# Who copies the table while the nodes are ranked: the first stage of a graph transformer, rearranged

## The chip, the cores and the metric

The kernel runs on one core of one Trainium2 chip. The metric is the device time of one execution in microseconds (us), the median of the runs; lower is better. The engines are TensorE (PE in the profile), VectorE (DVE), ScalarE (ACT), GpSimd (POOL) and SyncE (SP); 16 DMA engines move data.

## What is computed

Two layers of a heterogeneous graph transformer on 6250 nodes (128 numbers each, 16 node types) and 100,000 edges (32 edge types, sorted by destination), then a linear layer, a residual and a normalization:

```
def gt_layer(x, ntype, etype, src, dst, Wk, Wq, Wv, Wa, Watt, Wmsg, pri, skip, g, b):
    k = typed_linear(x, ntype, Wk).reshape(n, H, HS)          # H = 8, HS = 16
    q, v = ...                                                # the same with Wq, Wv
    kT = jnp.einsum('nhd,htdo->nhto', k, Watt)                # per node and edge type
    vT = jnp.einsum('nhd,htdo->nhto', v, Wmsg)
    a = jnp.einsum('ehd,ehd->eh', kT[src, :, etype], q[dst]) * pri[:, etype].T / SQRT_D
    att = edge_softmax(a, dst, n)
    hag = segment_sum((vT[src, :, etype] * att[:, :, None]).reshape(-1, H * HS), dst)
    h = silu(typed_linear(hag, ntype, Wa))
    alpha = sigmoid(skip[ntype])[:, None]
    h = h * alpha + x * (1.0 - alpha)
    return layernorm(h) * g + b
...
h = gt_layer(gt_layer(x, ...), ...)
return layernorm(x + (h @ ff_w + ff_b))
```

## The kernel before, in words

The kernel keeps one table per layer: for each node and each of the 32 edge types a row of 256 numbers, 128 of kT and 128 of vT. An edge then needs one gathered row.

**First stage** (up to `prep.close()`). Nodes are sorted by type (L337 to L389: the type counts, the place of each node, and the inverse order `inv`, by products on TensorE with one-hot tiles `row1` and `col1` that VectorE makes in three parts). After that the first layer's table is made, by a loop over the 16 types and over the 49 blocks of 128 sorted nodes (L952 to L966). `fetch` gathers x's rows on GpSimd's queue. `linears0` makes a type's `hT`, `kT` and `vT`: it moves over the columns shared with the type before (VectorE, L908), transposes, multiplies, and copies kT with ScalarE (L927) and vT with VectorE (L925). `table_block` makes each block in two pieces of 16 edge types (2.1 MB each), each in two halves (kT, then vT) of four products `tb` (L249). Each product is copied from PSUM to the piece's tile `st` by ScalarE (L256) or, where its number `hp` is in `share`, by VectorE (L254). After both halves `put0` scatters the piece to the table with an indirect DMA from GpSimd's queue (L938). There are four tiles `st` and five `tb`.

Beside the table the nodes are *ranked*: `rank_order` is a generator, and the loop resumes it between the halves. `degrees` counts each node's edges: 64 instructions that compare all of a partition's edges with one node number (L521), four to a group, with a few small ones to a group (`counts`, L493 to L508) and 8 products (`summed`). Then keys are made and counted (13 groups, L642), the classes' limits worked out, the ranks gathered (13 groups, L704 to L733), and number, start, degree and type of each ranked node are moved to their place (13 groups, L756 to L773). With the ranks known the generator says "gathers": for each of 49 blocks of ranked nodes GpSimd gathers the edges' row numbers (L803, `ell`), VectorE makes masks (L807), and GpSimd gathers x's rows (L815, `xr`) and stores them in the new order (L812, L821). At the end come the mixing factors and the limits that choose between a fast and a general program (L824 to L860).

Before the change the loop resumes the generator once to each half of a piece's making, every second half while it says "gathers". `share` is (1,) in odd blocks before that and in all blocks from then on, else empty.

**Edges.** Two passes (`edges`, L1036) gather table rows edge by edge (L1184) and do softmax, sums and the node work; the second layer's table is made beside the first pass.

The order of GpSimd's instructions is the order in which the program is written. On the other engines a scheduler orders the first stage's instructions by their dependencies and its own estimates; each engine then runs its list in order.

Of the kernel before, what the change touches and what calls it, by code (L numbers as in the profile page):

```python
# [13 lines left out]
ALU = mybir.AluOpType  # L14
# [4 lines left out]
P = 128  # L19
# [6 lines left out]
SB = 4  # L26
# [38 lines left out]
def kernel(  # L65
# [110 lines left out]

    def scale_edge_weights():

        nc.vector.tensor_scalar(prit, prit, 1.0 / float(HS) ** 0.5, None, op0=ALU.mult)
        nc.vector.tensor_tensor(bdk, bdk, prit.unsqueeze(2).to_broadcast([P, RT, 2 * HS]),  # L180
                                op=ALU.mult)

    def load_first():
        load_typed(wkqv[:, 0], Wk[0])
        load_typed(wkqv[:, 1], Wv[0])
        load_edge_weights(0)
        scale_edge_weights()

    def load_later():

# [9 lines left out]
    def superblocks(n):  # L200
        k = -(-n // SB)
        for c in range(k):
            yield n * c // k, n * (c + 1) // k - n * c // k

    def rows(ap, i0, k):
        return ap[i0 * P:(i0 + k) * P, :].rearrange("(i p) d -> p i d", p=P)
# [164 lines left out]
    for i0 in range(0, NT, 17):  # L371
        sl = slice(i0, min(i0 + 17, NT))
        k = sl.stop - sl.start
        nc.vector.tensor_tensor(col1[:, sl, 1], placeb[:, 1, sl].unsqueeze(2).to_broadcast([P, k, NT]),
                                colb[:, :NT].unsqueeze(1).to_broadcast([P, k, NT]), op=ALU.is_equal)
        nc.vector.tensor_tensor(col1[:, sl, 0], col1[:, sl, 1],
                                colb[:, sl].unsqueeze(2).to_broadcast([P, k, NT]), op=ALU.mult)
        nc.vector.tensor_scalar(col1[:, sl, 1], col1[:, sl, 1], rowf, None, op0=ALU.mult)
        nc.vector.tensor_tensor(row1[:, sl], placeb[:, 0, sl].unsqueeze(2).to_broadcast([P, k, P]),
                                colb.unsqueeze(1).to_broadcast([P, k, P]), op=ALU.is_equal)  # L380
        for i in range(sl.start, sl.stop):
            nc.tensor.matmul(inv_ps, row1[:, i], col1[:, i], start=(i == 0), stop=(i == NT - 1))
    inv2 = pp.tile([P, 2, NT], F32, name="inv2")
    nc.vector.tensor_copy(inv2, inv_ps)
    inv = pp.tile([P, NT], I32, name="inv")
# [2 lines left out]
    for tg in range(TG):  # L388
# [8 lines left out]
    nc.vector.tensor_copy(shift_t, first_t[:, 1])  # L397
    odd_t = pp.tile([P, 2, TY], F32, name="odd_t")
    nc.vector.tensor_tensor(odd_t[:, 0], first_t[:, 0], first_t[:, 1], op=ALU.not_equal)
    nc.vector.tensor_reduce(odd_t[:, 1], cnt_t.rearrange("p (t i) -> p t i", t=TY),  # L400
                            axis=AX.X, op=ALU.add)
# [69 lines left out]
    def degrees(got):  # L471

        rel = pp.tile([P, EC], F32, name="rel", tag="lo")
        nc.vector.tensor_scalar(rel, dsti, lowest, None, op0=ALU.subtract)
        nid = pp.tile([P, NEAR], I32, name="nid")
        nc.vector.tensor_scalar(nid, colf[:, :NEAR], lowest, None, op0=ALU.add)
        parts = pp.tile([P, 2, NEAR], I32, name="nidparts")
        nc.vector.tensor_single_scalar(parts[:, 0], nid, P - 1, op=ALU.bitwise_and)
        nc.vector.tensor_single_scalar(parts[:, 1], nid, 7, op=ALU.arith_shift_right)
        at = pp.tile([P, 2, NEAR], F32, name="nidat")  # L480
        nc.vector.tensor_copy(at, parts)
        yield
        near = pp.tile([P, NEAR], F32, name="near")
        same = pp.tile([P, EC], BF16, name="same_dst", tag="eti")
        deg_ps = pps.tile([P, NT], F32, name="ps")
        counted = []

        def counts(c0):


            sl = slice(c0, c0 + SB)
            whole = pp2.tile([P, SB], I32, name="whole")
            nc.vector.tensor_copy(whole, near[:, sl])  # L493
            part = pp2.tile([P, 2, SB], I32, name="part")
# [3 lines left out]
            nc.vector.tensor_tensor(ol, at[:, 0, sl].unsqueeze(2).to_broadcast([P, SB, P]),  # L498
                                    colf.unsqueeze(1).to_broadcast([P, SB, P]), op=ALU.is_equal)
            oh = pp2.tile([P, SB, NT], BF16, name="oh", tag="rh", bufs=1)  # L500
            nc.vector.tensor_tensor(oh, at[:, 1, sl].unsqueeze(2).to_broadcast([P, SB, NT]),
                                    colf[:, :NT].unsqueeze(1).to_broadcast([P, SB, NT]),
                                    op=ALU.is_equal)
            ov = pp2.tile([P, 2, SB, NT], BF16, name="ov", tag="ovb")
            for i in range(2):
                nc.vector.tensor_tensor(ov[:, i], oh,
                                        part[:, i].unsqueeze(2).to_broadcast([P, SB, NT]),
                                        op=ALU.mult)  # L508
            counted.append((c0, ol, ov))

        def summed():

            c0, ol, ov = counted.pop(0)
            for c in range(SB):
                for i in range(2):
                    nc.tensor.matmul(deg_ps, ol[:, c], ov[:, i, c], start=(c0 + c + i == 0),
                                     stop=(c0 + c == NEAR - 1 and i == 1))

        for c0 in range(0, NEAR, SB):
            for c in range(c0, c0 + SB):  # L520
                nc.vector.tensor_scalar(same, rel, float(c), None, op0=ALU.is_equal, op1=ALU.add,  # L521
                                        accum_out=near[:, c:c + 1])
            yield
            if counted:
                summed()
            counts(c0)
            if c0 % 8:
                yield
        yield
        summed()  # L530
        yield
        deg = pp.tile([P, NT], F32, name="deg")
        nc.vector.tensor_copy(deg, deg_ps)
        nc.vector.tensor_tensor(deg_far, deg_far, deg, op=ALU.subtract)
        nc.vector.scalar_tensor_tensor(deg, deg_far, far, deg, op0=ALU.mult, op1=ALU.add)
        yield from ordered(got, deg)
# [72 lines left out]
    with tc.manual_schedule(engines={mybir.EngineType.Pool}):  # L609

        def rank_order():
# [92 lines left out]
            for i0, k in superblocks(NT):  # L704
# [19 lines left out]
                for got, what in ((move, shifts), (room, limits)):  # L724
# [1 line left out]
                    nc.vector.tensor_tensor(to[:, :k], oc[:, :k],  # L726
                                            what.unsqueeze(1).to_broadcast([P, k, P]), op=ALU.mult)
                    nc.vector.tensor_reduce(got[:, i0:i0 + k], to[:, :k], axis=AX.X, op=ALU.add)
                yield
                to = pp2.tile([P, SB, P], F32, name="rl", bufs=1)  # L730
                nc.vector.tensor_tensor(to[:, :k], oc[:, :k], c_ps[:, :k], op=ALU.mult)
                nc.vector.tensor_reduce(rank[:, i0:i0 + k], to[:, :k], axis=AX.X, op=ALU.add)
# [64 lines left out]
            nc.sync.dma_start(typed, tyr)  # L797
            yield "gathers"

            stored = []  # L800
            for i0, k in superblocks(NB):
                for b in range(i0, i0 + k):
                    nc.gpsimd.indirect_dma_start(  # L803
                        out=ell[:, KO[b]:KO[b] + KB[b]], out_offset=None, in_=kvs[:],
                        in_offset=bass.IndirectOffsetOnAxis(ap=start[:, b:b + 1], axis=0))

                    nc.vector.tensor_scalar(neg[:, KO[b]:KO[b] + KB[b]], colf[:, :KB[b]],  # L807
                                            degr[:, b:b + 1], -BIG, op0=ALU.is_ge, op1=ALU.mult)
                    if (b - i0) % 2 or b == i0 + k - 1:
                        yield "gathers"  # L810
                if stored:
                    nc.gpsimd.dma_start(*stored.pop())  # L812
                xr = tp.tile([P, SB, D], F32, name="xr")
                for i in range(k):
                    nc.gpsimd.indirect_dma_start(  # L815
                        out=xr[:, i, :], out_offset=None, in_=x,
                        in_offset=bass.IndirectOffsetOnAxis(ap=some[:, i0 + i:i0 + i + 1], axis=0))
                    if i % 2 or i == k - 1:
                        yield "gathers"
                stored.append((rows(xrd, i0, k), xr[:, :k]))  # L820
            nc.gpsimd.dma_start(*stored.pop())  # L821
            yield "done"

            onehot = pp.tile([P, NB, TY], F32, name="onehot")  # L824
            nc.vector.tensor_tensor(onehot, meta[:, 3].unsqueeze(2).to_broadcast([P, NB, TY]),
# [126 lines left out]
        for t in range(TY):  # L952
# [4 lines left out]
            for b in range(b0, b1):  # L957
                def store(tg, st, b=b):
                    put0(st, tg, b)
                share = (1,) if stage in ("gathers", "done") or (not stage and b % 2) else ()  # L960
                for half, _ in enumerate(table_block(tp, tnb, *got[t], b - b0, share, STB0, store)):
                    next(beside, None)
                    if stage != "gathers" or half % 2:
                        stage = next(ranking, "done")
            for _ in beside:
                pass  # L966
# [634 lines left out]
```

## Time and profile before

| | us |
|---|---|
| median of 3 runs (lowest to highest) | 3328.6 (3323.8 to 3333.16) |
| profiled execution, its own time | 3324.49 |
| its span, first to last instruction | 3322.7 |
| first scatter of a table piece (L938) | 60.9 |
| last scatter of a table piece | 645.4 |
| first gather of the edges (L1184) | 667.3 |

Engines' busy shares of the span: PE 50%, DVE 58%, ACT 29%, POOL 73%. Granted TensorE clock, mean: 0.651.

How to read it: times in the views are us from the span's start; the mean of one instruction in a group is in ns. A row of a timeline has start, length, engine, line and operation, output<-inputs, and in brackets how long the engine was idle before it and what ended that. Scatters of table pieces are counted by L938. The lines are those of the kernel before; the changed kernel's stand up to 20 lines later.

### The profile page before, as it was taken

What the parts mean: (1) busy time and instruction counts of PE and PEld (TensorE: products, weight loads), DVE (VectorE), ACT (ScalarE), POOL (GpSimd) and SP (SyncE); (2) the same over time, 40 slices, a digit from 0 to 9 for tenths busy, and PEclk for the clock granted to TensorE, in tenths of its full rate; (3) what the DMA queues carried; (4) which work ended last, traced back from release to release, by engine and by line L of the source; (5) the groups of instructions that cost most, each with busy time, mean ns of one, the idle gap of its engine ahead of it and who ended that gap; (6) DMA issues with size and microseconds to landing.
All of it is one profiled execution on the core that took longest, in us unless ns stands there. A gap on an engine that the chain in (4) does not pass through costs nothing. (4 is left out here: it accounts for less than half of the span.)

```text
span 3322.7 us, 24680 instructions
## 1 busy us (share of the span) xinstructions
PE 1645.8 (50%) x5216; PEld 719.5 (22%) x5216; DVE 1925.0 (58%) x4361; ACT 974.6 (29%) x1599; POOL 2435.2 (73%) x5483
## 2 busy tenths in 40 slices
PE   3799899611477587665877589101201201113013
PEld 1344444300122133331333223000100101001001
DVE  8868522145556665666666662356556556666665
ACT  1565655400244235222352346101111111111111
POOL 2232565488788888888788881688888878888883
PEclk9788866555776587666787678555555555556555
DMA  6697899953477577665794679633333333333331
GB/s 151 264 414 326 363 400 403 392 127 92 133 262 252 193 275 269 213 209 167 253 349 162 206 282 391 218 106 110 105 103 107 108 95 109 108 106 104 101 98 40
DMA packets 170055, 678.46 MB, mean 204 GB/s; under 512 B 53292, under 2 KB 83790, under 8 KB 144846
## 3 DMA queue, kind: packets, MB, share of 16 engines
q0 software_dynamic: 115456, 642.08, 54.1%
q1 hardware_dynamic: 38050, 27.55, 2.9%
q10 hardware_dynamic: 16384, 7.11, 1.0%
q14 instruction: 120, 0.98, 0.1%
q8 instruction: 45, 0.74, 0.1%
HBM read 252.31 MB, written 425.02 MB: 204 GB/s over the span
## 5 line engine op out<-in xcount | busy, mean ns | idle before, releaser
L1184 POOL DMA_INDIRECT kv<-tab,ell x1666 | 1674.3, 1005 | 304.6 <-issue 256.8
L256 ACT COPY st<-tb 128x512 f32<-128x512 f32 (+1 forms) x1016 | 695.2, 759 | 550.2 <-PE tb L249 308.1
L1200 DVE TENSOR_TENSOR kv<-kv,tb 128x512 f32<-128x512 f32 (+3 forms) x227 | 145.9, 643 | 455.7 <-DMA kv<-tab,ell 445.8
L234 PE MATMUL nb<-ident,hag 128*128 128x128 f32 x98 | 25.8, 406 | 757.4 <-DVE hag L1238 757.4
L1200 DVE TENSOR_TENSOR kv<-kv,q 128x512 f32<-128x512 f32 (+3 forms) x227 | 146.2, 647 | 369.6 <-DMA kv<-tab,ell 364.0
L1190 POOL MEMSET pause<- 128x32 bf16 x3332 | 339.7, 141 | 0.7
L249 PE MATMUL tb<-bdv,kvT 32*128 32x512 f32 x784 | 280.1, 817 | 97.2 <-ACT st L256 96.5
L249 PE MATMUL tb<-bdv,vT 32*128 32x512 f32 x784 | 288.7, 847 | 62.6 <-DVE st L254 39.2
L1204 DVE TENSOR_REDUCE a<-kv 128x32 f32<-128x512 f32 (+3 forms) x454 | 287.4, 636 | 2.2
L938 POOL DMA_INDIRECT tab<-st,rows x98 | 100.4, 1024 | 253.7 <-ACT st L256 135.9
L249 PE MATMUL tb<-bdk,kvT 32*128 32x512 f32 x784 | 258.0, 806 | 18.2 <-ACT st L256 17.9
L249 PE MATMUL tb<-bdk,kT 32*128 32x512 f32 x784 | 238.3, 854 | 4.1 <-DVE st L254 4.1
L254 DVE COPY st<-tb 128x512 f32<-128x512 f32 (+1 forms) x160 | 116.3, 729 | 203.4 <-PE tb L249 124.8
L226 PE MATMUL nb<-xm,wa 128*128 128x512 f32 (+2 forms) x320 | 175.7, 705 | 92.5 <-DVE xm L212 92.2
L212 DVE SCALAR_TENSOR_TENSOR xm<-ntb,nb 128x512 f32<-128x512 bf16 (+2 forms) x288 | 157.1, 586 | 91.2 <-PE nb L234 79.7
L1399 POOL DMA_INDIRECT tab<-st,row x98 | 110.2, 1124 | 135.6 <-ACT st L256 107.6
L234 PEld LDWEIGHTS nb<-ident,hag 128*128 128x128 f32 x98 | 16.1, 202 | 774.3 <-issue 572.4
L226 PE MATMUL nb<-xm,wq 128*128 128x512 f32 (+2 forms) x160 | 91.1, 718 | 148.3 <-DVE xm L212 148.2
L1081 ACT COPY tb<-hq 128x128 f32<-128x128 f32 x49 | 13.1, 269 | 481.9 <-DVE sums L1124 423.0
L1350 PE MATMUL nb<-xm,wkqv 128*128 128x512 f32 (+1 forms) x288 | 148.2, 674 | 10.8 <-DVE xm L212 10.8
L249 PEld LDWEIGHTS tb<-bdv,vT 32*128 32x128 f32 x784 | 105.8, 236 | 158.7 <-ACT st L256 87.7
L234 PE MATMUL nb<-ident,hs 128*128 128x128 f32 x98 | 32.5, 463 | 211.0 <-DVE hs L1311 211.0
(291 smaller groups left out, 2731.3 us busy)
## 6 DMA issues: line engine op xcount, KB each, us to landing
kv<-tab,ell POOLq DMA_INDIRECT x1666
hr<-xrd SPq DMA_DIRECT2D x16, 256.0 KB, 3.6
hqd<-hs SPq DMA_DIRECT2D x8, 512.0 KB, 3.2
hq<-hqd SPq DMA_DIRECT2D x8, 512.0 KB, 3.9
xrd<-xr POOLq DMA_DIRECT2D x10, 256.0 KB
ntb<-typed SPq DMA_DIRECT2D x16, 128.0 KB, 3.3
hr<-xrd SPq DMA_DIRECT2D x10, 192.0 KB, 4.7
hqd<-hs SPq DMA_DIRECT2D x5, 384.0 KB, 3.0
```

Of the source, the lines that this page charges most:

```text
L212: nc.vector.scalar_tensor_tensor(xm[:, :n], ntb[:, :n], float(t), hT[:, :n], op0=ALU.is_equal, op1=ALU.mult)
L226: nc.tensor.matmul(ps[:, :n], w[:, t, :], xm[:, :n], start=(t == types[0]), stop=(t == types[-1]))
L249: nc.tensor.matmul(pt[:, b], yT[s, i * P:(i + 1) * P], bd[s, tt, :], start=True, stop=True)
L254: nc.vector.tensor_copy(to, pt)
L256: nc.scalar.copy(to, pt)
L938: put = nc.gpsimd.indirect_dma_start(out=tabs[0].rearrange("(n t) c -> n (t c)", t=16), out_offset=bass.IndirectOffsetOnAxis(ap=rows1[:, t ...
L1184: get = nc.gpsimd.indirect_dma_start(out=kv[:, j - j0, :], out_offset=None, in_=tabs[l][:], in_offset=bass.IndirectOffsetOnAxis(ap=ell[:, ...
L1190: nc.gpsimd.memset(pause[:, at % PAUSES, half], 0.0)
L1200: nc.vector.tensor_tensor(kk, kk, q.unsqueeze(1).to_broadcast([P, c, D]), op=ALU.mult)
L1204: nc.vector.tensor_reduce(a[:, j0:j1, :], kk.rearrange("p k (h d) -> p k h d", h=H), axis=AX.X, op=ALU.add)
L1350: nc.tensor.matmul(ps[:, :n], wkqv[:, j, t, :], xm[:, :n], start=(t == types[0]), stop=(t == types[-1]))
L1399: put = nc.gpsimd.indirect_dma_start(out=tabs[1].rearrange("(n t) c -> n (t c)", t=16), out_offset=bass.IndirectOffsetOnAxis(ap=row2[:, tg ...
```

## The change

1. Until the ranks are known `share` is empty: ScalarE makes all copies, but for block 0, where it is (1, 3) and VectorE makes half of them. From "gathers" on it is (1,) as before.
2. The generator is not resumed in block 0. After it, it is resumed at each half, also while it says "gathers".
3. Counting pauses after every two of L521's instructions, and again around `counts`; ranking pauses three times to a group instead of twice.
4. The mixing factors and the limits become a generator of their own, `limits_of`, which the gathers resume; they no longer come at the end.
5. `behind` gives the scheduler an order without a wait: the scaling of the edge weights, one sum for the limits and the comparisons in `counts` come after the last comparison of the sort.

```
-        scale_edge_weights()                       # in load_first
...
+    def behind(what, other):
+        tc.add_manual_dep(
+            what.ins, other.ins.name,
+            mybir.DependencyInfo(mybir.DependencyClass.NoSync,
+                                 mybir.DependencyReason.SCHED_ONLY),
+            reason="not wanted sooner")
...
-        nc.vector.tensor_tensor(row1[:, sl], placeb[:, 0, sl]...
+        sorted_by = nc.vector.tensor_tensor(
+            row1[:, sl], placeb[:, 0, sl]...
...
+    behind(scale_edge_weights(), sorted_by)
...
-    nc.vector.tensor_reduce(odd_t[:, 1], ...)
+    behind(nc.vector.tensor_reduce(odd_t[:, 1], ...), sorted_by)
...
-            nc.vector.tensor_tensor(ol, ...)      # and oh, in counts
+            behind(nc.vector.tensor_tensor(ol, ...), sorted_by)
...
             for c in range(c0, c0 + SB):
                 nc.vector.tensor_scalar(same, rel, float(c), None, ...)
-            yield
+                if c % 2:
+                    yield
             if counted:
                 summed()
-            counts(c0)
             if c0 % 8:
                 yield
+            counts(c0)
+            yield
...
                     nc.vector.tensor_reduce(got[:, i0:i0 + k], ...)   # ranking
-                yield
+                    yield
...
+            beside = limits_of(meta, full)
...                                                # at both yields of the gathers:
+                        next(beside, None)
                         yield "gathers"
...
             nc.gpsimd.dma_start(*stored.pop())
+            for _ in beside:
+                pass
             yield "done"
+
+        def limits_of(meta, full):
...
-                share = (1,) if stage in ("gathers", "done") or (not stage and b % 2) else ()
+                share = (1,) if stage in ("gathers", "done") else (1, 3) if b == 0 else ()
...
-                    if stage != "gathers" or half % 2:
+                    if b:
                         stage = next(ranking, "done")
```

More of the change, by code (lines that the diff above doesn't have):

```diff
@@ L177, in scale_edge_weights @@
     def scale_edge_weights():
-        nc.vector.tensor_scalar(prit, prit, 1.0 / float(HS) ** 0.5, None, op0=ALU.mult)
+        first = nc.vector.tensor_scalar(prit, prit, 1.0 / float(HS) ** 0.5, None, op0=ALU.mult)
         nc.vector.tensor_tensor(bdk, bdk, prit.unsqueeze(2).to_broadcast([P, RT, 2 * HS]),
                                 op=ALU.mult)
+        return first
     def load_first():
@@ L378 @@
         nc.vector.tensor_scalar(col1[:, sl, 1], col1[:, sl, 1], rowf, None, op0=ALU.mult)
-        nc.vector.tensor_tensor(row1[:, sl], placeb[:, 0, sl].unsqueeze(2).to_broadcast([P, k, P]),
-                                colb.unsqueeze(1).to_broadcast([P, k, P]), op=ALU.is_equal)
+        sorted_by = nc.vector.tensor_tensor(
+            row1[:, sl], placeb[:, 0, sl].unsqueeze(2).to_broadcast([P, k, P]),
+            colb.unsqueeze(1).to_broadcast([P, k, P]), op=ALU.is_equal)
         for i in range(sl.start, sl.stop):
             nc.tensor.matmul(inv_ps, row1[:, i], col1[:, i], start=(i == 0), stop=(i == NT - 1))
+    behind(scale_edge_weights(), sorted_by)
     inv2 = pp.tile([P, 2, NT], F32, name="inv2")
@@ L399 @@
     nc.vector.tensor_tensor(odd_t[:, 0], first_t[:, 0], first_t[:, 1], op=ALU.not_equal)
-    nc.vector.tensor_reduce(odd_t[:, 1], cnt_t.rearrange("p (t i) -> p t i", t=TY),
-                            axis=AX.X, op=ALU.add)
+    behind(nc.vector.tensor_reduce(odd_t[:, 1], cnt_t.rearrange("p (t i) -> p t i", t=TY),
+                                   axis=AX.X, op=ALU.add), sorted_by)
     nc.vector.tensor_scalar(odd_t[:, 1], odd_t[:, 1], float(WIN), None, op0=ALU.is_gt)
@@ L497, in counts @@
             ol = pp2.tile([P, SB, P], BF16, name="ol", tag="oc")
-            nc.vector.tensor_tensor(ol, at[:, 0, sl].unsqueeze(2).to_broadcast([P, SB, P]),
-                                    colf.unsqueeze(1).to_broadcast([P, SB, P]), op=ALU.is_equal)
+            behind(nc.vector.tensor_tensor(
+                ol, at[:, 0, sl].unsqueeze(2).to_broadcast([P, SB, P]),
+                colf.unsqueeze(1).to_broadcast([P, SB, P]), op=ALU.is_equal), sorted_by)
             oh = pp2.tile([P, SB, NT], BF16, name="oh", tag="rh", bufs=1)
-            nc.vector.tensor_tensor(oh, at[:, 1, sl].unsqueeze(2).to_broadcast([P, SB, NT]),
-                                    colf[:, :NT].unsqueeze(1).to_broadcast([P, SB, NT]),
-                                    op=ALU.is_equal)
+            behind(nc.vector.tensor_tensor(
+                oh, at[:, 1, sl].unsqueeze(2).to_broadcast([P, SB, NT]),
+                colf[:, :NT].unsqueeze(1).to_broadcast([P, SB, NT]), op=ALU.is_equal), sorted_by)
             ov = pp2.tile([P, 2, SB, NT], BF16, name="ov", tag="ovb")
@@ L818, in rank_order @@
                     if i % 2 or i == k - 1:
+                        next(beside, None)
                         yield "gathers"
```

## The prediction

> **What bounds the kernel now.** I read the page's slices first, then a table of stretches, the same table for the scatters alone, the timelines of VectorE and GpSimd, and last the groups. A "piece" is one of 98 blocks of 2.1 MB that the first stage scatters into the table (L938); a "step" is one resumption of the ranking; "counting" is the 64 compare-and-count instructions of L521.
>
> ```profile
> DMA  6697899953477577665794679633333333333331
> ...
> core 0: us, PE busy (x) PEld busy (x) DVE busy (x) ACT busy (x) POOL busy (x), PEclk, DMA share, GB/s
> 61.00:151.00 90.00, 56.69 (x288) 23.70 (x287) 85.76 (x260) 39.11 (x77) 17.21 (x20) 0.70 0.53 221
> 151.00:226.00 75.00, 72.72 (x341) 32.05 (x341) 38.59 (x91) 55.45 (x110) 22.71 (x26) 0.86 1.01 419
> 226.00:305.00 79.00, 73.04 (x279) 29.59 (x271) 73.40 (x134) 45.54 (x89) 20.69 (x24) 0.80 0.85 351
> 305.00:356.00 51.00, 46.63 (x237) 27.38 (x236) 36.65 (x101) 29.71 (x58) 12.43 (x14) 0.90 0.78 323
> 381.00:645.00 264.00, 238.02 (x803) 120.06 (x799) 77.71 (x123) 154.73 (x301) 161.20 (x174) 0.66 1.00 403
> 667.00:3323.00 2656.00, 1119.30 (x3123) 468.62 (x3123) 1552.38 (x3493) 628.82 (x924) 2169.09 (x5145) 0.63 0.51 170
> ```
> ```profile
> 61.00:151.00 90.00, 10.18 (x10) 0.70 0.53 221
> 151.00:226.00 75.00, 15.45 (x15) 0.86 1.01 419
> 381.00:645.00 264.00, 48.71 (x48) 0.66 1.00 403
> ```
>
> In the first table each row is a stretch: length, busy time by engine, granted clock, DMA share, GB/s. The second counts scatters. From 667 on the edges run; the change leaves the order of every instruction there as it is, so those 2656 us stay. Before that, the floor is the transfer: 15 pieces in 75 us with the DMA at 1.01 are 5.0 us each. From 61 to 151 only ten pieces go, because VectorE is busy 85.76 of 90 us (counting) while the odd blocks wait for it to copy a quarter of their results. From 226 to 356 the DMA is at 0.85 and 0.78. From 381 to 645 it is full again. What can be won is the idle DMA of 61 to 151 and of 226 to 381.
>
> **Sort first.**
>
> ```profile
> 15.88 0.68 DVE L498 TENSOR_TENSOR ol<-nidat,colf 128x512 bf16<-128x512 f32 x1
> 18.18 0.94 DVE L400 TENSOR_REDUCE odd_t<-sums_t 128x16 f32<-128x784 f32 x1
> 20.00 0.36 DVE L501 TENSOR_TENSOR oh<-nidat,colf 128x196 bf16<-128x196 f32 x1
> 29.89 1.22 DVE L180 TENSOR_TENSOR bdk<-bdk,prit 128x1024 f32<-128x1024 f32 x1
> 41.60 0.26 DVE L384 COPY inv<-ps 128x98 f32<-128x98 f32 x1 [1.47 <-PE ps L382]
> ...
> 45.71 0.97 DVE L521 TENSOR_SCALAR_CACHE_REDUCE same_dst<-rel 128x782 bf16<-128x782 f32 x1
> ...
> 46.72 0.97 DVE L521 TENSOR_SCALAR_CACHE_REDUCE same_dst<-rel 128x782 bf16<-128x782 f32 x1
> ...
> 55.58 0.69 DVE L925 COPY vT<-l 128x512 f32<-128x512 f32 x1 [0.69 <-PE l L922]
> ```
>
> Ahead of the sorted order's copy at 41.60 stand two L498 (0.68 each), one L400, one L501 and the scaling L180: 3.9 us. In the new program's order L400 still precedes the last product of the sort, and one L498 falls between the copy and what the first gather needs, 1.6 us. Saved: 2.3 us (bounds 0 and 3.9). The scaling then lies beside TensorE's 1.47 us. The first type's vT ends at 55.58 + 0.69 - 2.3 = 54.0.
>
> **First block.** VectorE now copies half of pieces 1 and 2 (eight copies), with counting between them. In the new program's order ten counting steps lie among them: 8 x 0.69, 10 x 1.01 (46.72 - 45.71), and 2 us for the small ones, so piece 2 leaves at 71.6 (0.69 is what the like copy of L925 takes; the 2 us are an estimate). ScalarE waits for VectorE here. From block 1 on ScalarE copies everything until the ranks are known.
>
> **Counting.** No piece waits for VectorE's copies any more, but the third type's pieces (from piece 11 on) need its vT, which VectorE copies in order, and in the new order all 64 counting steps stand ahead of that copy. After piece 2 there remain 48 x 1.01 = 48.5 us and some 6 us of small ones (two vT, the moves of old columns, two groups' comparisons): vT at 126, piece 11 at 128 (half a piece of copying later). Without that wait it would leave at about 111 (nine pieces of 4.43 us, below, after 71.6); so VectorE still keeps 17 us. Today pieces 1 to 10 go up to 151 and piece 11 just behind (x10 and x15 in the second table). Lead: 23 us; if VectorE is 5 us later or does not bind at all, 18 or 40.
>
> **Pieces 12 to 70.** Ranks now take 1.5 times the steps (counting 56 for 24, ranking 39 for 26, the rest as it was), so the first rank-dependent gather stands behind piece 70 instead of 46.
>
> ```profile
> 145.57 0.97 POOL L938 DMA_INDIRECT tab<-st,rows  x1 [3.16 <-ACT st L256]
> ...
> 189.87 0.97 POOL L938 DMA_INDIRECT tab<-st,rows  x1 [3.70 <-ACT st L256]
> ...
> 226.15 0.97 POOL L938 DMA_INDIRECT tab<-st,rows  x1 [4.40 <-ACT st L256]
> ...
> 241.19 1.01 POOL L938 DMA_INDIRECT tab<-st,rows  x1 [5.67 <-issue]
> ...
> 251.00 0.97 POOL L938 DMA_INDIRECT tab<-st,rows  x1 [4.56 <-DVE rl L726]
> ...
> 265.70 0.97 POOL L938 DMA_INDIRECT tab<-st,rows  x1 [5.46 <-issue]
> 276.56 1.02 POOL L938 DMA_INDIRECT tab<-st,rows  x1 [4.04 <-DVE hT L908]
> 291.63 0.98 POOL L938 DMA_INDIRECT tab<-st,rows  x1 [6.51 <-issue]
> 304.67 0.97 POOL L938 DMA_INDIRECT tab<-st,rows  x1 [6.78 <-ACT st L256]
> 355.79 0.97 POOL L938 DMA_INDIRECT tab<-st,rows  x1 [3.61 <-ACT st L256]
> ```
>
> The first two rows are pieces 10 and 20: with an empty queue a piece comes every 4.43 us. The next six bound blocks of two pieces while ranks are gathered: shared ones take 15.0, 14.7 and 15.1 us, those of ScalarE alone 9.8 and 10.9, that is 7.5 against 5.2 a piece. This contrast is the heart of the forecast: the new program has only the second kind, and its rank steps lie thinner. The last two rows are pieces 38 and 46, under the f32 products of L771 on TensorE: 6.4 each, unchanged. So: 9 x 4.43 = 40 (the queue fills), 23 x 5.0 = 115, 19 x 5.2 = 99, 8 x 6.4 = 51, in sum 305: piece 70 at 433 (today near 490: piece 50 at 381, then 5.5 each). Bounds: 5.0 throughout saves 10; the mean of both kinds, 6.5, in the ranking costs 26.
>
> **Denser gathers.** The 98 gathers of L803 and L815 must now go beside 26 pieces instead of 50, with four gathers to a piece on GpSimd's one queue.
>
> ```profile
> L938 POOL DMA_INDIRECT tab<-st,rows x49 | 50.0, 1021 | 30.5 <-DVE st L254 8.9 <-issue 7.3 <-ACT st L256 6.7
> L815 POOL DMA_INDIRECT xr<-in_x_dram,some x46 | 44.6, 969 | 35.2 <-DMA tab<-st,rows 24.4 <-issue 8.2 <-DMA ell<-kvs,start 1.7
> L803 POOL DMA_INDIRECT ell<-kvs,start x46 | 44.2, 960 | 28.2 <-DMA tab<-st,rows 11.6 <-issue 9.8 <-DMA xr<-in_x_dram,some 6.8
> ...
> L812 POOL DMA_DIRECT2D xrd<-xr x12 | 9.9, 825 | 2.6 <-issue 1.4 <-DMA tab<-st,rows 1.2
> ```
>
> With 0.30 us between issues: 98 x 1.27 + 26 x 1.32 + 12 x 1.13 = 172, and one fetch, 173 us: 6.7 a piece, above the transfer's 5.0, so GpSimd becomes the bound here. Above, with the idle that L815 and L803 have now (1.73 and 1.57 each), it is 209. I take 182, near the lower end, because those idles end with a landed scatter, and scatters will be further apart. Transfers ask less: 48 pieces in 264 us are 5.5, so 0.5 a piece is what gathers and stores add, 24 us in all, and 26 x 5.0 + 24 = 154. VectorE's steps behind the ranks (the masks of L807, the mixing factors, the limits that used to come last) cost nothing: it has 78 busy us in the 264, and GpSimd's eleven issues up to the first scatter that needs a VectorE copy take 14 us; without that cover it would be some 5 us, once.
>
> **End of the stage.**
>
> ```profile
> 644.17 0.95 POOL L815 DMA_INDIRECT xr<-in_x_dram,some  x1 [0.30 <-issue]
> 645.43 1.02 POOL L938 DMA_INDIRECT tab<-st,rows  x1 [0.30 <-issue]
> 657.70 0.81 POOL L821 DMA_DIRECT2D xrd<-xr  x1 [11.24 <-DMA xr<-in_x_dram,some]
> ...
> 667.32 0.99 POOL L1184 DMA_INDIRECT kv<-tab,ell  x1 [8.81 <-DMA wkqv<-in_L_gnn_Wv_dram]
> ```
>
> Today 23 us pass from the last gather of x to the first of the edges. The new order has the last store, and behind it pieces 97 and 98: GpSimd waits in that store for the landing (7 us, one scatter ahead of it, where today's 13.5 has two), then 2 x 1.3 us of issue, 10 us of transfer and about 3 of landing and branch: 24. Sum: 433 + 1 + 182 + 24 = 640 against 667, 27 us sooner. The profiled execution took 3324.5 us (span 3322.7) and becomes 3297.5; the median of the runs lies 4.1 us above it, so 3301.
>
> **Rivals.**
> - The DMA bounds everything (chance 0.12): the vT wait vanishes in queued work (piece 11 at 111) and the ranking holds 5.0. For it: 419 GB/s whenever nothing waits. Against it: the order on VectorE. Piece 70 at 406, and with 173 the edges start at 604: 3324.5 - 63 + 4 = 3266.
> - TensorE takes VectorE's place (0.11): it is busy 0.92 of the ranking at a clock of 0.80 and runs in order, so ScalarE alone is fed only every 5.8 us in pieces 21 to 62. For it: the 6.4 of pieces 38 to 46. Against it: 5.2 in the blocks of ScalarE alone. 42 x 5.8 = 244 for 214: +30, 3331, no change. The change would then not do what it says.
> - Transfers bound the dense part (0.03): at 0.8 us of the queue to a gather it takes 26 x 5.0 + 98 x 0.8 = 208, +26 on my 182: 3327, no change. Against it: 24 us for some 104 gathers and stores now, 0.23 each. The Trainium skill ("DMA: Bandwidth & Descriptors", Bandwidth) speaks for it: 0.95 us of transfer for 64 KB, 0.68 for 4 KB, by which, as an estimate, the 98 gathers would take 80 us. The trace's 0.23 disagrees, hence the low chance.
> - GpSimd stands in the dense part (0.16), slower: each of 12 stores of x waits in GpSimd's queue for its last gather's landing, and every later scatter stands behind. For it: the last store's 11.24 us of idle. If a landing takes 13.5 us as there, and six issues (7.7 us) lie between, each store waits 5.8 us, 70 us less the 9 already in the sum: 3301 + 61 = 3362. It decides from 3.0 us of wait each on. Against it: L812's first twelve stores now waited 2.6 us in all, at a full DMA.
>
> **Numbers.** My forecast has 0.58 (its own range 3283 to 3318, by the bounds above), the rivals 0.12, 0.11, 0.03 and 0.16. About 0.3%, 10 us, is what a measurement of this kernel can tell. Faster is the forecast and the first rival, 0.70; same, the second and third, 0.14; slower 0.16. The range 3275 to 3335 takes in the second and third and leaves out the slower one and the far end of the first.
>
> **What would show it.** Right: piece 2 near 71, piece 11 near 128, piece 70 near 433; no VectorE copies of the kind of L254 between piece 3 and piece 72; DMA near 1.0 from 130 to 380; gathers 1.3 us apart after 435; the edges' first gather near 640. Wrong: ScalarE's waits on TensorE growing while the DMA falls below 0.9 (second rival), or idle of several us before each store of x (fourth); or a different length after the edges begin.

## The result, and the profile after

The changed kernel took 3292.8 us (median; 3288.4 to 3299.2) against 3328.3 us before: ratio 0.9894, 95% interval 0.9871 to 0.9918, about 35 us faster. The forecast was 3301, in a range of 3275 to 3335. The profiled execution took 3289.7 us with a span of 3287.8.

The 40 slices of the page come first: the share of the DMA in tenths, in slices of 82 us. Slice 2 now has 8 where it had 6, and slices 4 and 5 have 9 where they had 7 and 8. Slice 6 has 8 for 9.

```profile
DMA  6899989933566587565785589433333333333331
```

The same table of stretches as for before, cut at the same times as far as the stages allow (columns: stretch, length, busy time by engine with instructions, granted clock, DMA share, GB/s):

```profile
core 0: us, PE busy (x) PEld busy (x) DVE busy (x) ACT busy (x) POOL busy (x), PEclk, DMA share, GB/s
61.00:127.00 66.00, 54.00 (x207) 26.46 (x208) 64.53 (x179) 40.14 (x80) 16.96 (x21) 0.71 0.78 324
127.00:171.00 44.00, 44.00 (x203) 19.82 (x200) 15.02 (x48) 38.39 (x78) 12.95 (x15) 0.90 0.94 389
171.00:226.00 55.00, 54.25 (x239) 26.73 (x236) 13.35 (x34) 45.83 (x93) 19.91 (x23) 0.86 1.01 417
226.00:305.00 79.00, 78.99 (x343) 37.26 (x342) 38.42 (x90) 64.32 (x130) 24.85 (x28) 0.84 1.00 419
305.00:356.00 51.00, 50.23 (x207) 22.67 (x204) 36.25 (x63) 41.44 (x84) 15.79 (x19) 0.95 1.01 419
437.00:611.00 174.00, 142.02 (x444) 72.21 (x444) 44.92 (x100) 87.19 (x171) 131.62 (x139) 0.60 0.92 349
640.00:3287.00 2647.00, 1120.70 (x3119) 470.00 (x3119) 1550.51 (x3490) 629.50 (x923) 2163.66 (x5133) 0.62 0.51 171
```

The stretch with the counting now ends near 127, with the DMA at 0.78 where 61 to 151 had 0.53. From 226 to 356 the DMA is at 1.00 and 1.01 where it was 0.85 and 0.78. The new cost is the dense part, 437 to 611: 0.92 where the part with gathers had 1.00.

GpSimd's timeline at the points that the prediction named (start, duration, instruction, idle before it and who ended it); L958 is the scatter of a piece, L817 the first rank-dependent gather, L830 the last gather of x, L837 the last store of x, L1204 the edges:

```profile
70.26 0.99 POOL L958 DMA_INDIRECT tab<-st,rows  x1 [6.94 <-issue]
...
119.15 0.98 POOL L958 DMA_INDIRECT tab<-st,rows  x1 [14.53 <-ACT st L264]
...
126.83 1.49 POOL L958 DMA_INDIRECT tab<-st,rows  x1 [2.35 <-ACT st L264]
...
170.75 0.98 POOL L958 DMA_INDIRECT tab<-st,rows  x1 [5.55 <-ACT st L264]
...
432.48 1.29 POOL L958 DMA_INDIRECT tab<-st,rows  x1 [4.25 <-ACT st L264]
...
437.13 0.95 POOL L817 DMA_INDIRECT ell<-kvs,start  x1 [0.16 <-issue]
...
609.31 0.95 POOL L830 DMA_INDIRECT xr<-in_x_dram,some  x1 [0.30 <-issue]
620.24 0.80 POOL L837 DMA_DIRECT2D xrd<-xr  x1 [9.98 <-DMA xr<-in_x_dram,some]
621.35 1.01 POOL L958 DMA_INDIRECT tab<-st,rows  x1 [0.30 <-issue]
622.66 1.00 POOL L958 DMA_INDIRECT tab<-st,rows  x1 [0.30 <-issue]
634.76 1.01 POOL L1204 DMA_INDIRECT kv<-tab,ell  x1 [11.10 <-SPq L1617]
```

These are pieces 2, 10, 11, 20 and 70, then the dense part and the end. The edges begin at 634.8 where they began at 667.3: 32.5 us. What follows lasted 2653.0 us against 2655.4. So nearly the whole gain lies in the first stage, and below each experiment is read by the start of its edges, and by its time beside it. Two executions of the changed kernel began the edges at 634.8 and 640.9, so a difference of less than some 6 us between single executions is not read as an effect.

### The profile page after: what moved, and what is told of

Its sections match the earlier page's. It is cut to its first block, busy times and chain, and to the rows that moved or that the text cites. A ratio compares the mean times of both kernels' runs of the same rounds, so it can differ in the third digit from the quotient of the medians.

```text
span 3287.8 us, 24649 instructions
## 1 busy us (share of the span) xinstructions
PE 1640.1 (50%) x5216; PEld 725.5 (22%) x5216; DVE 1872.2 (57%) x4273; ACT 1013.9 (31%) x1687; POOL 2434.6 (74%) x5483
## 5 line engine op out<-in xcount | busy, mean ns | idle before, releaser
L1204 POOL DMA_INDIRECT kv<-tab,ell x1666 | 1671.8, 1003 | 305.7 <-issue 259.5
L264 ACT COPY st<-tb 128x512 f32<-128x512 f32 (+1 forms) x1104 | 734.6, 760 | 478.2 <-PE tb L257 232.8
L958 POOL DMA_INDIRECT tab<-st,rows x98 | 100.9, 1030 | 261.9 <-ACT st L264 234.5
L257 PE MATMUL tb<-bdv,vT 32*128 32x512 f32 x784 | 274.2, 793 | 29.7 <-ACT st L264 25.8
L234 PE MATMUL nb<-xm,wa 128*128 128x512 f32 (+2 forms) x320 | 183.3, 732 | 93.7 <-DVE xm L220 93.4
L257 PE MATMUL tb<-bdk,kT 32*128 32x512 f32 x784 | 227.7, 801 | 1.7 <-DVE st L262 1.7
L1370 PE MATMUL nb<-xm,wkqv 128*128 128x512 f32 (+1 forms) x288 | 147.4, 671 | 11.5 <-DVE xm L220 11.5
L257 PEld LDWEIGHTS tb<-bdv,vT 32*128 32x128 f32 x784 | 107.0, 223 | 126.8 <-ACT st L264 100.3
L262 DVE COPY st<-tb 128x512 f32<-128x512 f32 (+1 forms) x72 | 55.9, 779 | 138.2 <-PE tb L257 81.4
```

The source lines that it names most:

```text
L234: nc.tensor.matmul(ps[:, :n], w[:, t, :], xm[:, :n], start=(t == types[0]), stop=(t == types[-1]))
L257: nc.tensor.matmul(pt[:, b], yT[s, i * P:(i + 1) * P], bd[s, tt, :], start=True, stop=True)
L264: nc.scalar.copy(to, pt)
L958: put = nc.gpsimd.indirect_dma_start(out=tabs[0].rearrange("(n t) c -> n (t c)", t=16), out_offset=bass.IndirectOffsetOnAxis(ap=rows1[:, t ...
L1204: get = nc.gpsimd.indirect_dma_start(out=kv[:, j - j0, :], out_offset=None, in_=tabs[l][:], in_offset=bass.IndirectOffsetOnAxis(ap=ell[:, ...
L1370: nc.tensor.matmul(ps[:, :n], wkqv[:, j, t, :], xm[:, :n], start=(t == types[0]), stop=(t == types[-1]))
```

## The experiments

Three groups, each beside the kernel before on its own chip (3323.0, 3555.3 and 3314.6 us there). The chip of the second group needed 2879 to 2900 us for the edges that take 2640 to 2655 on the others; times of that group are compared within it, and the first stage by its own rows. "Edges" is the start of the edges' first gather in the one profiled execution. The kernel before was profiled once, on the chip of the result. As an estimate, its 3323.0 us on the first group's chip, less the 2644 to 2650 us that the edges took there, put its edges at 671 to 677 on that chip, 4 to 10 us later than in the table; differences from 667.3 in the first group are uncertain by that much.

| kernel | piece 11 | piece 70 | edges | time against before (95% interval) |
|---|---|---|---|---|
| before | 151.2 | 489.4 | 667.3 | 1 |
| changed | 126.8 | 432.5 | 634.8 | 0.9894 (0.9871 to 0.9918) |
| 1: the share rule alone | 148.5 | 473.4 | 651.5 | 0.9914 (0.9892 to 0.9935) |
| 1: changed, old share rule | 148.6 | 474.9 | 679.9 | 1.0011 (0.9994 to 1.0027) |
| 1: changed, two gathers to a piece | 126.8 | 433.5 | 661.4 | 0.9981 (0.9960 to 1.0001) |
| 1: before, four gathers to a piece | 155.9 | 534.8 | 694.2 | 1.0049 (1.0029 to 1.0068) |
| 2: changed, counting held | 115.7 | 423.8 | 633.1 | 0.9913 (0.9885 to 0.9942) |
| 2: changed, three gathers to a piece | 127.2 | 433.8 | 638.8 | 0.9907 (0.9877 to 0.9937) |
| 2: two-step ranking, three gathers | 127.3 | 445.6 | 635.4 | 0.9907 (0.9875 to 0.9938) |
| 2: both, counting held | 110.6 | 433.2 | 621.0 | 0.9881 (0.9838 to 0.9924) |
| 3: changed, again | 127.4 | 437.8 | 640.9 | 0.9923 (0.9902 to 0.9945) |
| 3: stores of x on SyncE | 127.7 | 434.3 | 618.7 | 0.9844 (0.9822 to 0.9867) |
| 3: counting held, stores on SyncE | 115.2 | 425.6 | 610.2 | 0.9816 (0.9789 to 0.9842) |
| 3: all four | 111.0 | 435.1 | 619.1 | 0.9837 (0.9811 to 0.9863) |

**The share rule alone**, put into the kernel before:

```diff
-share = (1,) if stage in ("gathers", "done") or (not stage and b % 2) else ()
+share = (1,) if stage in ("gathers", "done") else ()
```

> The kernel before with one part of the change: from the second block on ScalarE alone copies pieces until the ranks are known; steps, sort and gather density stay old. Measured by when the edges' first gather starts (before 667.3, after 634.8). Theory A (VectorE's turn in the copies is what held pieces 21 to 37 back, and TensorE's sums behind VectorE's counting still hold pieces 1 to 10): piece 11 at about 143 (VectorE loses some ten copies of 0.75 us), the pieces of the ranking at 5.1 instead of 7.5 us in the odd blocks, piece 46 at 332, then 5.5 a piece as before: edges at 643, time about 3304. Rival (ScalarE alone is fed only every 5.8 us by TensorE): piece 46 at about 355, edges at 665, no change. Rival (the thinner steps bring the gain, not the share): piece 46 within 5 us of 355.

Edges at 651.5: 15.8 of the 32.5 us, and 8 us short of the expectation. By the time the share rule is worth more: 0.9914 lies between the changed kernel's 0.9894 and its repeat's 0.9923, and the intervals overlap. That the rest of the change adds to it is read from the edges alone, 17 and 11 us later here than in the changed kernel's two executions. The waits of TensorE from 62 to 151 (who waited, for whom; us in all, times, longest), before and with the share rule, show why piece 11 hardly moved:

```profile
PE tb L249 <- DVE st L254: 33.3, 4, 14.3
```
```profile
PE ps L516 <- DVE ov L506: 27.0, 6, 6.7
```

L254 is VectorE's copy of a product, L516 the sums of the counting, L506 their operands. With the copies gone from VectorE, TensorE waits nearly as long for the counting itself, and behind that wait stand the pieces: in the old steps the sums come before VectorE has their operands. The pieces of the ranking did go faster: pieces 20 to 38 from 192.7 to 287.3, 5.3 each (before: 6.4).

**The old share rule in the changed kernel:**

```diff
-share = (1,) if stage in ("gathers", "done") else (1, 3) if b == 0 else ()
+share = (1,) if stage in ("gathers", "done") or (not stage and b % 2) else (1, 3) if b == 0 else ()
```

> The changed kernel with the old rule put back from the second block on: in odd blocks VectorE copies a quarter of the pieces until the ranks are known. Theory A: each odd block of the counting and ranking costs some 2 x 2.3 us over one of ScalarE alone where VectorE's ranking work stands in front of the copies (pieces 13 to 56, half of them odd: 22 x 2.3 = 50, less what the thinner steps leave free, so 15 to 40): piece 70 at 450 to 470, edges at 650 to 675. Rival (the thinner steps alone free VectorE, so that the share costs nothing): piece 70 within 5 us of 432, edges near 635.

Edges at 679.9, 45 us later than in the changed kernel (39 later than in its repeat): beyond the upper end of theory A. Against the kernel before they are 13 us later in the table, but the time is the same (1.0011, with 1 inside the interval). One row of TensorE's timeline and two stretches hold most of it:

```profile
119.95 2.08 PE L257 MATMUL tb<-bdv,vT 32*128 32x512 f32 x4 [15.74 <-DVE st L262]
```
```profile
62.00:151.00 89.00, 66.35 (x223) 29.59 (x221) 74.27 (x198) 39.24 (x75) 17.91 (x21) 0.59 0.59 243
...
187.00:388.00 201.00, 186.18 (x779) 84.01 (x776) 110.50 (x222) 135.32 (x266) 60.59 (x68) 0.81 0.97 402
```

TensorE waits 15.74 us for one copy of VectorE's that stands behind the counting; piece 11 is 22 us later. Pieces 20 to 56 then take 5.6 us each (187.2 to 387.8) where the changed kernel takes 5.05 (170.8 to 352.7), 19 us more. So the thinner steps and the dense gathers bring nothing without the share rule. By the start of the edges the share rule is worth more with them (39 to 45 us) than without (16); the times, 1.0011 to 0.9894 or 0.9923 with them and 1 to 0.9914 without, do not show that difference clearly.

**Two gathers to a piece in the changed kernel:**

```diff
-if b:
+if b and (stage != "gathers" or half % 2):
     stage = next(ranking, "done")
```

> The changed kernel with the old density of the rank-dependent gathers, two to a piece for four. Theory A (GpSimd's issues bound the dense part at 1.27 us each): 28 pieces at 5.5 us (the transfers bind again) = 154 from 437, then some 42 gathers and 5 stores alone on GpSimd, 59 us, and a short end of 6: edges at 656, 21 us later than with four to a piece. Rival B (transfers bound the dense part): edges within 5 us of 635, because the same bytes go. Rival C (the waits of the stores of x bind): fewer gathers between store and landing, so edges later than 665.

Edges at 661.4, 5 us behind theory A (656). Two stretches, and the last gather and the start of the edges:

```profile
437.00:585.00 148.00, 128.24 (x448) 66.34 (x446) 46.02 (x105) 88.20 (x173) 86.04 (x92) 0.69 1.00 404
585.00:661.00 76.00, 0.00 (x0) 0.00 (x0) 0.19 (x2) 0.00 (x0) 49.34 (x54) 0.50 0.39 124
```
```profile
654.29 0.94 POOL L830 DMA_INDIRECT xr<-in_x_dram,some  x1 [0.30 <-issue]
...
661.44 0.97 POOL L1204 DMA_INDIRECT kv<-tab,ell  x1 [3.22 <-SPq L1617]
```

The DMA is full (1.00) until piece 98 leaves at 584.0, 39 us sooner than with four, and then at 0.39: GpSimd is left alone with the last 46 gathers. The same bytes go, and the edges come 21 us later, so rival B fails.

**Four gathers to a piece in the kernel before:**

```diff
-if stage != "gathers" or half % 2:
+if True:
     stage = next(ranking, "done")
```

> The kernel before with one part of the change: the rank-dependent gathers four to a piece. Theory A: up to piece 46 nothing moves (355.8); then GpSimd binds for 25 pieces (173 to 182 us from 362) with a DMA share near 0.92, and 27 pieces at 5.0 follow (135): with a shorter end of about 13 us for 22, because no gather stands in the last pieces, edges at 668 (662 to 680): no change. So the density brings nothing by itself. Rival (the density is what brings the gain): edges at 640 to 650.

A miss: 0.5% slower, edges at 694.2. The stretches and the end:

```profile
362.00:551.00 189.00, 159.37 (x495) 78.15 (x491) 55.02 (x105) 92.79 (x179) 147.62 (x160) 0.63 0.86 331
551.00:675.00 124.00, 114.65 (x383) 66.01 (x381) 30.21 (x46) 80.64 (x155) 27.93 (x31) 0.64 1.01 418
675.00:694.00 19.00, 0.00 (x0) 0.00 (x0) 0.97 (x2) 0.33 (x2) 0.85 (x1) 0.50 1.00 382
```
```profile
674.88 0.97 POOL L938 DMA_INDIRECT tab<-st,rows  x1 [3.85 <-ACT st L256]
694.23 1.00 POOL L1184 DMA_INDIRECT kv<-tab,ell  x1 [18.39 <-DMA wkqv<-in_L_gnn_Wk_dram]
```

Piece 98 left at 674.9, as the terms add up (362, 178 and 135). But these terms and the end of 13 make 688, not the 668 that the expectation gives: most of the miss is in its adding, and 6 us in the end, for with no gather in the last pieces the DMA still had 19 us of issued pieces to work off, not 13. Of the 26.9 us against 667.3, 6.4 stood there already at piece 46 (362.2 for 355.8), ahead of every gather, where nothing was expected to move; whether the chip or the scheduler's order does that is open. From piece 46 on the stage is 20.5 us longer, and the DMA's idle time in the dense part (0.14 of 189 us, 26 us) is enough for that. So density by itself costs; in the change it is the price of ranks that come later.

**Counting held back** in the changed kernel: each counting instruction is placed behind the sums' operands of two groups before.

```diff
+one = nc.vector.tensor_scalar(same, rel, float(c), ...)
+if len(paced) >= 2:
+    behind(one, paced[-2])
```

> The changed kernel with one thing more: VectorE's counting instructions are held, so that each group's counting starts only behind the sums' operands of two groups before; the order on VectorE is then four counting steps, one group's operands, four counting steps, and the third type's vT comes in between; TensorE's and ScalarE's order stay. Theory A (the 9.7 and 1.9 us that TensorE waits for VectorE at pieces 10 and 11 are lost transfer time that nothing gives back): piece 10 at 108 for 119.1, piece 11 at 113 for 126.8, piece 70 at 421 for 432.5, edges at 624 for 634.8. Rival (VectorE has no slack before 128, so the held counting shows up as waits of TensorE for the sums of pieces 12 to 25): piece 11 earlier, but piece 26 at 193 to 197 as now, and edges at 632 to 637.

In the changed kernel TensorE's timeline has these two waits:

```profile
111.81 0.72 PE L527 MATMUL ps<-ov,ol 128*128 128x49 bf16 x8 [9.71 <-DVE ov L517]
...
122.42 2.09 PE L257 MATMUL tb<-bdv,vT 32*128 32x512 f32 x8 [1.91 <-DVE vT L945]
```

With the counting held they are gone, and two stretches of it read:

```profile
62.00:127.00 65.00, 64.87 (x270) 33.22 (x267) 43.07 (x137) 51.84 (x103) 19.77 (x23) 0.81 0.89 366
435.00:625.00 190.00, 165.60 (x417) 71.90 (x415) 39.97 (x63) 86.14 (x160) 129.19 (x137) 0.64 0.86 330
```

Piece 11 came 11 us sooner and piece 70 still 8.7, so the first half of theory A holds. The kernel with three gathers, below, ran on this chip and is the changed kernel's program up to the first gather: beside its 127.2 and 433.8 the lead is 11.5 and 10.1. The edges came only 1.7 us sooner than in the changed kernel: in the dense part GpSimd now waited 13.5 us for copies of ScalarE's (1.5 in the changed kernel), and the DMA is at 0.86 of 190 us where the changed kernel has 0.92 of 174. Whether the chip or the shifted start does that is open, for the changed kernel's dense part was not run on this chip. In the third group, with the stores moved, the same edit carried 8.5 us to the edges.

**Three gathers to a piece**, and the same with **two-step ranking** (the `yield` behind each of two rank gathers moved out of their loop), so that the ranks are known after piece 64:

```diff
-if b:
+if b and (stage != "gathers" or half != 3):
     stage = next(ranking, "done")
```

> The changed kernel with three rank-dependent gathers to a piece for four (two gathers at three of four places of a block). In GpSimd's order 12 gathers and 4 stores then stand behind piece 98. Theory A (GpSimd's issues bind at four, the transfers at 5.7 us a piece with three, both balanced; what then stands behind the last piece hides its backlog): piece 98 at 593, edges at 621. Rival (GpSimd's total of 98 gathers x 1.27 us is the bound however it is spread): edges within 4 us of 635. Rival (like two to a piece: what stands behind the last piece costs): 640 or later.

> The changed kernel with the rank gathers in the old two steps for three a group, so that the ranks are known behind piece 64 for 70, and the rank-dependent gathers three to a piece, so that they end right before piece 98. Theory A (in the ranking VectorE and TensorE have room since ScalarE copies alone, so the denser steps cost at most 5 us): first gather at 399 to 404, 34 pieces x 5.7 = 194, edges at 612 (608 to 618). Rival (the thinner steps were what kept the DMA full from 226 to 356): a piece of the ranking takes 5.8 us or more, first gather at 412 or later, edges at 625 or later.

Neither brought anything: 638.8 and 635.4. In the first I had miscounted: 22 gathers stand behind piece 98 (597.0), not 12, and GpSimd needs until 631.6 to issue the last. The rival, GpSimd's total, holds (638.8, within its 4 us of 635). In the second the idle DMA only moved:

```profile
356.00:435.00 79.00, 66.99 (x309) 34.50 (x311) 47.99 (x133) 47.31 (x94) 30.64 (x33) 0.87 0.84 343
435.00:625.00 190.00, 159.82 (x491) 79.22 (x486) 46.43 (x74) 99.71 (x187) 129.37 (x138) 0.65 0.98 383
```

0.98 in the dense part, but 0.84 from 356 to 435: the first gather left at 412.9, as its rival had it, not at 399 to 404. The rival's reason fails, though: from 226 to 356 the DMA stayed at 1.01, and pieces 20 to 56 took 5.1 us each. The time was lost after them: pieces 56 to 64 took 6.5 each (5.3 in the changed kernel).

**Both together with the held counting:**

> The held counting, the two-step rank gathers and three gathers to a piece together. Theory A (the three gains lie one behind the other, none hides another: the DMA is the floor of all): edges at 602 (597 to 610), time 33 us under the changed kernel's. Rival (the first gain is given back by a DMA that is full from 127 on): edges at 612 as without the held counting.

Edges at 621.0, 12 to 14 us before each of its parts, and 19 later than the sum that I expected. Against 0.9907 and 0.9913, the ratio 0.9881 is no clear difference.

**The changed kernel again, and the stores of x on SyncE's queue:**

```diff
-nc.gpsimd.dma_start(*stored.pop())
+nc.sync.dma_start(*stored.pop())
```

> The changed kernel unaltered, as the measure for the other runs of this group and for how far the first stage repeats: piece 11 at 127, piece 70 at 433, first rank-dependent gather at 437, edges at 635, each within 4 us. If the dense part differs from chip to chip as the edges do, edges at 640 to 650.

> The changed kernel with the 13 stores of x on SyncE's queue for GpSimd's. Theory A (GpSimd's queue bounds the dense part: 13 issues of 1.13 us, 3.9 us of waits, and the 10 us that it stands in the last store with pieces 97 and 98 behind): last gather at 592 for 609, pieces 97 and 98 right behind it, edges at 614 (609 to 619), 20 us sooner. Rival (the DMA is the floor there, busy 0.92 of 190 us, so at most 15 us can be won and the landing of the last pieces takes most of it): edges at 628 to 633. Rival (the stores are hidden): no change.

The repeat missed its expectation: piece 11 came at 127.4, but piece 70 at 437.8 and the edges at 640.9, 5 and 6 us behind the first execution. The dense part is the same (172.9 us from the first gather to the last, 172.2 in the first execution). The difference arises between pieces 46 and 50, which took 26.2 us for 20.1. The stretch in the first execution and in the repeat:

```profile
302.00:322.00 20.00, 20.00 (x90) 9.11 (x82) 15.71 (x28) 16.93 (x35) 7.43 (x9) 1.00 1.02 418
```
```profile
302.00:322.00 20.00, 20.00 (x66) 9.38 (x65) 10.90 (x19) 12.61 (x26) 6.85 (x8) 0.64 0.98 401
```

TensorE is busy all the time in both, at a granted clock of 1.00 and of 0.64, and 35 copies of ScalarE's became 26.

With the stores on SyncE's queue the edges begin at 618.7, 22 us sooner than in the repeat beside it; time 3264.0 against 3289.1. Of the 22, 3.7 us are there already at the first gather (438.8 for 442.5; the granted clock from 302 to 322 was 0.90), so some 18 belong to the stores. This shows that GpSimd's queue binds the dense part. The stretch, and the end of GpSimd's timeline:

```profile
435.00:600.00 165.00, 136.12 (x459) 70.15 (x457) 48.53 (x119) 90.45 (x178) 125.89 (x134) 0.68 0.99 383
```
```profile
596.81 0.95 POOL L830 DMA_INDIRECT xr<-in_x_dram,some  x1 [0.30 <-DMA tab<-st,rows]
598.06 1.01 POOL L958 DMA_INDIRECT tab<-st,rows  x1 [0.30 <-issue]
599.38 1.01 POOL L958 DMA_INDIRECT tab<-st,rows  x1 [0.30 <-issue]
618.69 1.00 POOL L1204 DMA_INDIRECT kv<-tab,ell  x1 [18.31 <-ACTq L1617]
```

With 13 issues and their waits gone, the DMA rises from 0.92 to 0.99, and the last gather leaves at 596.8 (615.3 in the repeat). Then the transfers bind, and the backlog of 18 us at the end cannot be hidden any more. The Trainium skill ("DMA: Bandwidth & Descriptors", Issuing engine by pattern) gives simple loads and stores to SyncE and indirect ones to GpSimd; this run agrees, by some 18 us.

> The held counting and the stores of x on SyncE's queue together. Theory A: the two lie one behind the other: piece 70 at 424, edges at 605 (599 to 610). Rival (what is won in the counting is lost again in the dense part, as the held counting alone ended at 633): edges at 612 or later.

> The held counting, two-step rank gathers, three gathers to a piece, and the stores of x on SyncE's queue. Without the last part the edges began at 621, with the DMA the bound from piece 65 on. Theory A (the DMA is the floor there, so freeing GpSimd brings little): edges at 614 to 621. Rival (GpSimd's queue still binds): 605 to 611.

Counting held and stores on SyncE: edges at 610.2, 3256.1 us, ratio 0.9816 with an upper end (0.9842) below the lower end of the changed kernel's repeat (0.9902). It is the fastest, 33 us below the changed kernel, though its lead over the stores alone (8 us) lies within the intervals; the rows that carry that lead are piece 11 (115.2 for 127.7) and piece 70 (425.6 for 434.3). The edges fall just behind theory A's range (599 to 610) and ahead of the rival's 612. With the two-step ranking and three gathers added the edges begin at 619.1, 9 us later and inside theory A's 614 to 621: beside the 621.0 with the stores on GpSimd's queue, freeing GpSimd brings little. The times of the two (0.9816 and 0.9837) are no clear difference.

## Why the prediction was right

**Sort first.** The first type's vT was forecast to end at 54.0 and ended at 53.3 (start 52.62, 0.69 long).

**First block.** Piece 2 at 71.6, measured 70.3; VectorE's copies of L262 stand between 54.9 and 68.8, and the next at 441.6.

**Counting.** vT of the third type at 126, measured 122.3; piece 11 at 128, measured 126.8. The size was right, the name half right: of TensorE's wait, 9.71 us go to the sums' operands and 1.91 to vT. Both are the order of counting ahead of them, as the held counting showed. "VectorE still keeps 17 us" was 11 to 16: with the counting held piece 11 left at 115.2 to 115.7, and at 110.6 to 111.0 with two-step ranking on top. Why that ranking, whose steps come after piece 11, moves it was not tried.

**Pieces 12 to 70.** 305 us forecast, 305.7 measured. The terms: pieces 12 to 20 took 43.9 (forecast 40), 21 to 43 114.1 (115), 44 to 62 99.7 (99), 63 to 70 47.9 (51). The sum is closer than its terms, and the repeat took 310.4, so that it came within 1 us is in part luck. The contrast of odd and even blocks, 7.5 against 5.2, carried it: ScalarE alone kept 5.05 a piece from 20 to 56. (The bound's "mean of both kinds, 6.5" should be 6.35, 22 us and not 26.) TensorE was busy 0.99 of 171 to 353 while the DMA was at 1.00, so the second rival was not far off: here it did not bind, but in the repeat, at a granted clock of 0.64, it cost some 6 us between pieces 46 and 50.

**Denser gathers.** This is the mis-sized term. I took 182 us between the ends 173 and 209; from the first gather to the last it was 172.2 (437.13 to 609.31), the low end. A gather with its idle time had cost GpSimd 1.73 and 1.57 us (L815 and L803, of it 0.97 and 0.96 the instruction); now the same two cost 1.27 and 1.25, so most of the idle time vanished. The groups of the stretch 436 to 611 (by line: instructions, busy and mean, idle before them and what ended it):

```profile
L830 POOL DMA_INDIRECT xr<-in_x_dram,some x49 | 47.2, 963 | 14.9 <-issue 13.1 <-DMA xrd<-xr 1.5 <-DVE deepest L880 0.3
L817 POOL DMA_INDIRECT ell<-kvs,start x49 | 46.7, 953 | 14.6 <-issue 13.1 <-DMA tab<-st,rows 0.6 <-DMA xr<-in_x_dram,some 0.6
L958 POOL DMA_INDIRECT tab<-st,rows x26 | 26.5, 1019 | 7.9 <-issue 6.4 <-ACT st L264 1.5
L827 POOL DMA_DIRECT2D xrd<-xr x12 | 9.7, 812 | 3.9 <-DMA xr<-in_x_dram,some 3.8
```

What is left is about 0.30 us between issues. Between piece 70 and the first gather 4.6 us passed for 1 forecast, for two fetches stand there.

**End of the stage.** 24 us forecast, 25.5 measured; the stand in the last store was 10.0 for 7.

In sum 634.8 for 640: 9.8 us less in the dense part and 0.5 at piece 70, 3.6 more ahead of the first gather and 1.5 at the end. The time came out 8 us below the 3301: 5 us of these are here, 2.4 are the edges, which were to stay the same, and 1 is the distance of the median from the profiled execution (3.1 for 4.1). That errors of both signs met in the sum is luck; the mechanism does not rest on it.

**The rivals.** The DMA does not bind everything: 0.78 while counting, 0.92 in the dense part. It would have begun the edges at 604; even the best version here begins them at 610. Transfers do not bind the dense part of the changed kernel: with the stores moved to SyncE's queue, 28 pieces and 98 gathers took 165.1 us (434.3 to 599.4), that is 0.26 a gather over 5.0 a piece, near the 0.23 of before. The 80 us that I estimated from the Trainium skill ("DMA: Bandwidth & Descriptors", Bandwidth) would have made it 220. The slower rival, GpSimd standing in twelve stores, needed 3.0 us each: they waited 3.9 us together (L827 above). Five issues lie between the last gather of four blocks and their store in GpSimd's order, only one of them a scatter, and the DMA is not full there; that the gathers had landed by then fits, but was not tried by itself. The stores still cost some 18 us, by their 13 issues and the stand at the end.

Not tried by themselves are the moved limits, the order given by `behind`, and block 0 without steps of the ranking.

## What to carry to other kernels

Compare blocks that differ in one rule within the profile of the kernel at hand (odd and even here): that contrast gave the 5.2 us a piece (measured 5.05) that no average showed. Price the parts of a change together, not one by one: the rest of the change brought nothing without the share rule (1.0011), and with it the edges began 11 to 17 us sooner than with the share rule alone. And where a stage turns from a full transfer queue to a full issue queue, look for issues that another engine's queue could take; moving 13 of them brought the edges some 18 us forward, beside the 32 of the whole change.

## What the runs showed of the hardware

A rank-dependent gather costs the DMA 0.26 us in a full queue, but GpSimd 1.25 us (0.95 and 0.30 between issues), so their number binds and not their bytes. One chip took 2879 to 2900 us for the edges that others do in 2640 to 2655, while its first stage, bound by large scatters, came to piece 70 at 433.8 (with three gathers, the same program up to there) where the others had 432.5, 437.8 and 434.3. And the clock granted to TensorE for the same stretch of the same program was 1.00 in one execution and 0.64 in another, which there delayed the pieces by 6 us.
